# Layer 0's weighted sum by rows: which operand stays in TensorE, and the gate's second half on VectorE

## The chip, the cores and the metric

The kernel runs on one core of a Trainium2 chip. The metric is device time in microseconds (us) of one execution. A core has engines that each take their own queue of instructions in order: TensorE (PE; its weight loads are listed apart, as PEld), VectorE (DVE), ScalarE (ACT) and GpSimd (POOL). SyncE (SP) issues transfers; GpSimd can issue them too, from its own queue. TensorE writes to PSUM[...]; the other data lie in SBUF, 128 partitions wide.

## The reference

Four graph layers run on x (16 batches of 1024 nodes and 128 features) with a 0/1 adjacency matrix of 1024 by 1024 for each batch. After each, the result is added to x and normalized by rows. The change touches layer 0 alone, which for each batch computes

```
h = x @ W_w.T + W_b
e = (h @ A) @ h.T;  e = e + e.T
att = softmax(where(adj > 0, e, -9e15), axis=1) * adj
h_prime = relu(att @ h)
coeff = sigmoid([x, h_prime] @ gate_w.T + gate_b)
x = layernorm(x + coeff * x + (1 - coeff) * h_prime)
```

The gate has one number for each node: a product of 256 weights with the node's 128 features of x and its 128 features of h_prime. Layer 1 thins the adjacency row by row (the dilation, a sequential process of eight column blocks here) and runs three aggregation steps; layer 2 is an attention like layer 0 with three gates; layer 3 is two graph convolutions. A general path, taken where the inputs are not what the fast path assumes, stands behind a flag and is not run.

## The kernel before, in words

The fast path is `fast_kernel`. Layer 0 has three generators for each batch:

- `before` (L922) loads x as `xn` (eight blocks of 128 nodes, nodes on partitions) and the adjacency by rows as `an`, turns it into an fp8 copy `Y` on ScalarE, checks its symmetry on VectorE against TensorE's turned copy (L943, L944), turns x into `xT` (features on partitions), and makes `G` (for the scores), `hn` (h by rows) and `gx` (the gate's product with x, by way of `gates`, L769). Its last step stores Y from GpSimd (L965).
- `attention` (L967) goes through eight blocks `jt` of 128 neighbours: scores by `wide_matmul` (L724), mask and extreme on VectorE (L983), exp on ScalarE (L985), then `hs`, the block of h divided by the sum of exp (L989). One step later `weigh` (L970) adds the block to `acc`. Here hs is the operand that is loaded into TensorE, and em, the exp's 1024 columns, is moved through it in two halves of 512. The result is h_prime turned: features on partitions, nodes along the columns.
- `after` (L998) takes the ReLU into `hpT`, forms the gate's product with it in `gates` (four matmuls, a copy by ScalarE, two turns), the tanh that stands for the sigmoid, then xn times its factor, hpT turned back to rows by eight transposes (`turned`, L754) and times its factor, their sum, and `normed` (L787): statistics on VectorE, the power -1/2 on GpSimd (L745), scale and shift on ScalarE (L801). GpSimd then stores the result (L1019).

`in_rounds` (L815) sets the order in which the three are written: a `yield n` puts the generator's next piece n rounds later. In iteration b run `before` of batch b+1, `attention` of b and `after` of b-1 together, in about 18 rounds. The written order isn't the order on the engines: a scheduler orders each engine's instructions before the run, with the written order as priority and its own estimate of when each is ready. What is written later may therefore come earlier where its engine is free.

Buffers: three for xn, so that the load of batch b+1 takes the place of batch b-2 and must wait until that has been stored; three for an; two each for the scores' PSUM tile and for em; one for acc, which ReLU must have read before the next batch's first sum; two PSUM banks (`ps_h`) for all small products and turns. All loads of x and of the adjacency go out on SP's queue.

After layer 0 comes the dilation, in which `prepare`, `fixed_point` and `removal` alternate. Its small tiles are in the pool `dl_small`. Layer 0's last `after` runs beside its first steps, and L1188, the power -1/2 of the node degrees on GpSimd, is ready as soon as the last scores are.

Of the kernel before, what the change touches and what calls it, by code (L numbers as in the profile page):

```python
# [9 lines left out]
F32 = mybir.dt.float32  # L10
# [5 lines left out]
FP8 = mybir.dt.float8e4  # L16
# [6 lines left out]
P = 128  # L23
# [616 lines left out]
def fast_kernel(ctx: ExitStack, tc: tile.TileContext, t: dict, out: bass.AP, flag: bass.AP):  # L640
# [46 lines left out]
    def nat(ap):  # L687
        return ap.rearrange("(t p) d -> p t d", p=P)
# [39 lines left out]
    def tiles3(ap):  # L728
        return ap.rearrange("p (t d) -> p t d", d=P)
# [53 lines left out]
    def half_rows(v):  # L783

        return v[:, :, None].to_broadcast([P, 4, P])
# [124 lines left out]
    work = ending.enter_context(tc.tile_pool(name="l0_work", bufs=1, reuse_waits="tile"))  # L910
    small = ending.enter_context(tc.tile_pool(name="l0_small", bufs=2, reuse_waits="tile"))
    b0 = row_bcast(wts, t["L0_gnn_W_b"], P, "l0brow")
    gw = wts.tile([P, 2, 32], F32, name="l0gw")
    nc.vector.memset(gw, 0.0)
    with nc.allow_non_contiguous_dma(reason="a vector of 256"):
        nc.sync.dma_start(gw[:, :, 0], t["L0_gnn_gate_w"].rearrange("o (h d) -> d (o h)", d=P))
    gb = row_bcast(wts, t["L0_gnn_gate_b"], 1, "l0gb")
    gbh = wts.tile([P, 1], F32, name="l0gbh")
    nbig = wts.tile([P, 1], F32, name="l0nbig")
# [2 lines left out]
    def before(s, b):  # L922

        s.xn = work.tile([P, NT, P], F32, name="xn", bufs=3)
        nc.sync.dma_start(s.xn, nat(t["x"][b]))
        yield 1
        for it in range(NT):
            c = b * NT + it
# [22 lines left out]
            if it == (4 if b else 1):  # L951
                s.G = work.tile([P, N], F32, name="G", bufs=2)
                for p, c in products(ps_h, (M0, s.xT)):
                    nc.scalar.activation(s.G[:, c], p, AF.Identity, scale=-1.0, bias=nu)
                pz = gates(ps_h, early.tile([P, N], FP8, name="chk").bitcast(F32), (gw[:, 0, :], s.xT))
                s.gx = small.tile([P, NT], F32, name="gx")
                nc.vector.tensor_copy(s.gx.rearrange("p (q t) -> p q t", t=2), pz[:, :, :, 0])
            if it == (5 if b else 2):
# [8 lines left out]
    def attention(s, b):  # L967
        s.acc = ps_a.tile([P, N], F32, name="acc")

        def weigh(jt, hs, em):  # L970
            for h in range(H2):
                c = slice(h * 512, (h + 1) * 512)
                nc.tensor.matmul(s.acc[:, c], hs, em[:, c], start=(jt == 0), stop=(jt == NT - 1))  # L973

        for jt in range(NT):
            js = slice(jt * P, (jt + 1) * P)
            c = b * NT + jt
            mn = mx0[:, c:c + 1]
            msk = work.tile([P, N], BF16, name="msk", bufs=2)
            nc.scalar.activation(msk, Y[b][:, jt, :], AF.Identity, scale=-BIG, bias=nbig)  # L980
            e = wide_matmul(ps_w, s.G[:, js], s.xT)
            em = work.tile([P, N], F32, name="em", bufs=2)
            nc.vector.tensor_tensor_reduce(em, e, msk, 1.0, 3.0e38, op0=OP.add, op1=OP.min, accum_out=mn)  # L983
            sm = small.tile([P, 1], F32, name="sm")
            nc.scalar.activation(em, em, AF.Exp, scale=-1.0, bias=mn, accum_out=sm)  # L985
            rs = small.tile([P, 1], F32, name="rs")
            nc.vector.reciprocal(rs, sm)
            hs = small.tile([P, P], F32, name="hs")
            nc.vector.tensor_scalar(hs, s.hn[:, js], rs, None, op0=OP.mult)  # L989
            yield  # L990
            if jt:
                weigh(*late)
            late = jt, hs, em
            yield
        weigh(*late)
        yield

    def after(s, b):  # L998

        hpT = work.tile([P, N], F32, name="hpT")  # L1000
        nc.scalar.activation(hpT, s.acc, AF.Relu)
        yield 3
        pz = gates(ps_h, work.tile([P, NT, P], F32, name="r").rearrange("p t d -> p (t d)")[:, :N // 4], (gw[:, 1, :], hpT))
        co = small.tile([P, NT], F32, name="co")
        nc.vector.tensor_add(co.rearrange("p (q t) -> p q t", t=2), pz[:, :, :, 0],
                             s.gx.rearrange("p (q t) -> p q t", t=2))
        nc.scalar.activation(co, co, AF.Tanh, scale=0.5, bias=gbh)
        cx = small.tile([P, NT], F32, name="cx")
        nc.vector.tensor_scalar(cx, co, 0.5, 1.5, op0=OP.mult, op1=OP.add)
        nc.vector.tensor_scalar(co, co, -0.5, 0.5, op0=OP.mult, op1=OP.add)  # L1010
        yield 3
        r = work.tile([P, NT, P], F32, name="r")
        nc.vector.tensor_mul(s.xn, s.xn, per_row(cx))
        for p, c, k in turned(ps_h, hpT):
            nc.vector.tensor_mul(r[:, k, :], tiles3(p), half_rows(co[:, k]))
        nc.vector.tensor_add(s.xn, s.xn, r)
        yield 4
        normed(small, s.xn)
        nc.gpsimd.dma_start(nat(x1_d[b]), s.xn)  # L1019
        yield  # L1020
# [13 lines left out]

    with ExitStack() as ph:
        sb = ph.enter_context(tc.tile_pool(name="dl_sb", bufs=2, side="right", reuse_waits="tile"))
        tiny = ph.enter_context(tc.tile_pool(name="dl_small", bufs=3, side="right", reuse_waits="tile"))
        ps_b = ph.enter_context(tc.tile_pool(name="dl_pb", bufs=1, space=PSUM, side="right", reuse_waits="tile"))
        ps_d = ph.enter_context(tc.tile_pool(name="dl_pd", bufs=1, space=PSUM, side="right", reuse_waits="tile"))
        ps_s = ph.enter_context(tc.tile_pool(name="dl_ps", bufs=2, space=PSUM, side="right", reuse_waits="tile"))  # L1040
# [826 lines left out]
```

## Time and profile before

| | |
|---|---|
| median of 3 runs | 2696.75 us (2693.25 to 2697.32) |
| the profiled execution | 2694.93 us; its span 2693.2 us |
| TensorE busy, of the span | 2539.0 us (94%) |
| VectorE | 2085.4 us (77%) |
| ScalarE | 1977.5 us (73%) |
| GpSimd | 317.7 us (12%) |
| layer 0: first to last record of its sums (L973) | 27.8 to 624.3 us |
| dilation: first and last column write (L1157) | 649.8 to 1001.2 us |
| layer 1's aggregations (L1307), first to last | 1005.7 to 1562.7 us |
| layers 2 and 3 (L1679, L1619) | from 1692.8 us to the end |
| mean granted TensorE clock | 0.983 of full speed |

The profile lists instructions by source line; a line can be a helper's, so L759 is every transpose by `turned`, and the names (out<-in) tell which. A float32 matmul appears as two records. The busy time of a matmul reaches to its modelled end, which overlaps its successor; the distance from one start to the next is what it costs the queue. A note in square brackets is idle time of the engine before the instruction, with what ended it. Stages have different limits, so the share of the whole span says little of one stage.

### The profile page before, as it was taken

How to read it: one execution, taken by the hardware profiler on the slowest of the kernel's cores; microseconds unless marked ns; L12 is line 12 of the kernel's file. 1: busy time of each engine (PE TensorE's matmuls, PEld its weight loads, DVE VectorE, ACT ScalarE, POOL GpSimd, SP SyncE). 2: the span in 40 equal slices, each digit the busy share in tenths (PEclk: the TensorE clock that was granted, in tenths of full speed). 3: DMA queues.
4: the chain of work that ended last, by engine and by line, in shares of the span. 5: the costliest groups of instructions: out<-in, count | busy, mean ns of one | idle time of the engine just before them, and what ended most of it. 6: DMA issues, size and time to landing. Idle time of an engine off the chain costs nothing.

```text
span 2693.2 us, 41450 instructions
## 1 busy us (share of the span) xinstructions
PE 2539.0 (94%) x14888; PEld 1677.9 (62%) x14888; DVE 2085.4 (77%) x5590; ACT 1977.5 (73%) x3188; POOL 317.7 (12%) x287
## 2 busy tenths in 40 slices
PE   8999999997888869999999998999999999999986
PEld 4444454444666648887788885566566666666655
DVE  6887778876898877777688875678778777887885
ACT  7888889885988866666655534777777777777773
POOL 0000000003000001111122132001100100001010
PEclk9999999998999989999999998999999999999998
DMA  6555555530000052233366673102122111111100
GB/s 191 157 180 172 164 172 168 168 121 21 2 3 2 2 212 87 95 118 128 132 230 238 228 263 132 40 32 79 67 85 77 63 63 63 63 63 63 47 24 25
DMA packets 120807, 285.34 MB, mean 106 GB/s; under 512 B 12304, under 2 KB 65424, under 8 KB 113424
## 3 DMA queue, kind: packets, MB, share of 16 engines
q1 hardware_dynamic: 101280, 203.33, 23.1%
q0 software_dynamic: 19312, 79.28, 7.6%
q8 instruction: 119, 1.95, 0.3%
q14 instruction: 96, 0.79, 0.1%
HBM read 202.72 MB, written 79.82 MB: 105 GB/s over the span
## 4 chain that ended last, share of the span: by engine, by line
PE 58%; DVE 16%; issue 6%; ACT 4%; POOL 4%; DMA 2%; POOLq 0%; ACTq 0%; DVEq 0%
PE ph L1619 8%; PE acc L1679 7%; PE acc L1307 7%; PE ph L766 5%; PE acc L973 5%; PE pmm L724 5%; PE ph L759 4%; PE ph L1433 4%; PE pmm L1691 3%; PE ph L1606 2%; DVE mid L1097 2%; DVE keep L1148 2%; POOL ln_rstd L745 1%; POOL rn L745 1%; ACT q L1145 1%
## 5 line engine op out<-in xcount | busy, mean ns | idle before, releaser
L745 POOL TENSOR_TENSOR ln_rstd<-ln_rstd,mhalf 128x8 f32<-128x8 f32 (+1 forms) x68 | 108.3, 1593 | 1318.7 <-DVE ln_rstd L742 864.2
L973 PE MATMUL acc<-em,hs 128*128 128x512 f32 x512 | 259.3, 607 | 2.5 <-DVE past L1075 1.3
L724 PE MATMUL pmm<-xT,G 128*128 128x512 f32 x512 | 259.8, 604 | 0.0
L1679 PE MATMUL acc<-ex,hs 128*128 128x512 f32 x512 | 248.9, 596 | 7.5 <-DVE hs L1706 4.6
L801 ACT ACTIVATE xn<-xn,ln_nb,ln_rstd 128x128 f32<-128x128 f32 x512 | 204.6, 481 | 61.1 <-DVE ln_nb L799 61.0
L1307 PE MATMUL acc<-a,hi 128*128 128x512 f32 x768 | 232.7, 396 | 11.5 <-DVE a L1294 8.5
L1307 PE MATMUL acc<-a,lo 128*128 128x512 f32 x768 | 230.3, 394 | 5.9 <-DVE lo L1274 5.8
L985 ACT ACTIVATE em<-em,mx 128x1024 f32<-128x1024 f32 x128 | 146.3, 1143 | 54.0 <-DVE mx L983 52.7
L983 DVE CUSTOM_DVE_ANT_0 em<-pmm,msk 128x1024 f32<-128x1024 f32 x128 | 156.1, 1219 | 31.9 <-PE pmm L724 30.8
L1699 ACT ACTIVATE ex<-em,mn 128x1024 f32<-128x1024 f32 x128 | 146.9, 1148 | 44.7 <-DVE mn L1696 44.0
L1691 PE MATMUL pmm<-G,hT 128*128 128x512 f32 (+3 forms) x416 | 175.3, 523 | 0.1
L1696 DVE CUSTOM_DVE_ANT_0 em<-pmm,msk 128x1024 f32<-128x1024 f32 x128 | 155.4, 1214 | 24.4 <-PE pmm L1693 22.3
L1307 PEld LDWEIGHTS acc<-a,lo 128*128 128x128 f32 x768 | 143.1, 189 | 41.2 <-DVE lo L1274 12.0
L1307 PEld LDWEIGHTS acc<-a,hi 128*128 128x128 f32 x768 | 141.8, 189 | 42.9 <-DVE a L1294 11.0
L1157 ACT ACTIVATE carry<-pc,negone 128x1024 fp8e4<-128x1024 f32 x128 | 141.4, 1116 | 26.2 <-PE pc L1156 23.2
L931 ACT ACTIVATE carry<-an 128x1024 fp8e4<-128x1024 f32 x128 | 134.5, 1051 | 30.5 <-DMA an<-in_adj 29.7
L980 ACT ACTIVATE msk<-carry,l0nbig 128x1024 bf16<-128x1024 fp8e4 x128 | 145.4, 1136 | 0.0
L1619 PE MATMUL ph<-A,hi 128*128 128x512 f32 x512 | 143.1, 420 | 1.2 <-DVE zn L1608 0.7
L1687 ACT ACTIVATE msk<-A,nbig 128x1024 bf16<-128x1024 fp8e4 x128 | 144.2, 1137 | 0.0
L1296 ACT CAST a<-A 128x1024 fp32r<-128x1024 fp8e4 x96 | 98.4, 1048 | 54.3 <-PE acc L1307 52.7
L1679 PEld LDWEIGHTS acc<-ex,hs 128*128 128x128 f32 x512 | 88.6, 190 | 76.8 <-issue 54.6
L1296 ACT CAST a<-carry 128x1024 fp32r<-128x1024 fp8e4 x96 | 99.1, 1047 | 47.1 <-PE acc L1307 46.8
(319 smaller groups left out, 6185.2 us busy)
## 6 DMA issues: line engine op xcount, KB each, us to landing
an<-in_adj SPq DMA_DIRECT2D x128, 512.0 KB, 3.7
adj_d<-carry POOLq DMA_DIRECT2D x16, 1024.0 KB, 4.2
A<-dil_d SPq DMA_DIRECT2D x16, 1024.0 KB, 5.3
rdeg<-rdeg_d SPq DMA_DIRECT2D x32, 512.0 KB, 3.9
A<-adj_d SPq DMA_DIRECT2D x16, 1024.0 KB, 4.8
ag_d<-ag POOLq DMA_DIRECT2D x24, 512.0 KB, 5.0
ag<-ag_d SPq DMA_DIRECT2D x24, 512.0 KB, 5.3
xn<-in_x SPq DMA_DIRECT2D x16, 512.0 KB, 4.4
```

The lines of the kernel that those rows point to most:

```text
L724: nc.tensor.matmul(p[:, h * 512:(h + 1) * 512], lhsT, rhs[:, h * 512:(h + 1) * 512], start=True, stop=True)
L745: nc.gpsimd.tensor_tensor(r, r, mhalf[:, :n], op=OP.pow)
L801: nc.scalar.activation(r[:, k.start + i, :], r[:, k.start + i, :], AF.Identity, scale=rstd[:, i:i + 1], bias=nb[:, i:i + 1])
L973: nc.tensor.matmul(s.acc[:, c], hs, em[:, c], start=(jt == 0), stop=(jt == NT - 1))
L983: nc.vector.tensor_tensor_reduce(em, e, msk, 1.0, 3.0e38, op0=OP.add, op1=OP.min, accum_out=mn)
L1296: nc.scalar.copy(a, A[:, 2 * i:2 * i + 2, c])
L1307: nc.tensor.matmul(acc, part[:, jt, :], pieces[h * NT // 2 + k][:, jt - 2 * k, :], start=(part is parts[0] and jt == 0), stop=(part is par ...
L1619: nc.tensor.matmul(p, part[:, jt, :], A[jt][:, c], start=(jt == 0 and i == 0), stop=(jt == NT - 1 and i == 1))
L1679: nc.tensor.matmul(s.acc[:, c], hs, ex[:, c], start=(jt == 0), stop=(jt == NT - 1))
L1691: nc.tensor.matmul(e[:, c], s.hT[:, js], s.G[:, c], start=True, stop=True)
L1696: nc.vector.tensor_tensor_reduce(row, e, msk, 1.0, 0.0, op0=OP.add, op1=OP.min, accum_out=mn)
L1699: nc.scalar.activation(ex, row, AF.Exp, scale=-1.0, bias=mn, accum_out=sm)
```

## The change

- `weigh` swaps the operands: each of the eight 128-column blocks of em is loaded into TensorE and hs (128 columns) is moved through it. The sum comes out by rows: nodes on partitions, eight blocks of 128 features. The first of each four blocks in a PSUM bank carries the start flag of the bank.
- `after` takes the ReLU by rows into `hp`. The gate's half is a product with `ghrow` (the 128 weights, repeated on all partitions) and a sum along the features, on VectorE. Gate matmuls, copy and turns for h_prime are gone. hp is multiplied by its factor in SBUF, at full width.
- The pieces of `after` stand at rounds 0, 6, 9 and 17 in place of 0, 3, 6 and 10.
- From batch 3 on, x is loaded from GpSimd's queue.
- The gate's columns in `gw` are only x's; `ghrow` is one more load. Pool `dl_small` has two buffers of each tile in place of three.

```diff
-    gw = wts.tile([P, 2, 32], F32, name="l0gw")
+    gw = wts.tile([P, 32], F32, name="l0gw")
     nc.vector.memset(gw, 0.0)
-    with nc.allow_non_contiguous_dma(reason="a vector of 256"):
-        nc.sync.dma_start(gw[:, :, 0], t["L0_gnn_gate_w"].rearrange("o (h d) -> d (o h)", d=P))
+    nc.sync.dma_start(gw[:, 0:1], t["L0_gnn_gate_w"][:, :P].rearrange("o d -> d o"))
+    ghrow = row_bcast(wts, t["L0_gnn_gate_w"][:, P:], P, "l0gh")
...
-        nc.sync.dma_start(s.xn, nat(t["x"][b]))
+        (nc.gpsimd if b > 2 else nc.sync).dma_start(s.xn, nat(t["x"][b]))
...
-                pz = gates(ps_h, early.tile([P, N], FP8, name="chk").bitcast(F32), (gw[:, 0, :], s.xT))
+                pz = gates(ps_h, early.tile([P, N], FP8, name="chk").bitcast(F32), (gw, s.xT))
...
         def weigh(jt, hs, em):
-            for h in range(H2):
-                c = slice(h * 512, (h + 1) * 512)
-                nc.tensor.matmul(s.acc[:, c], hs, em[:, c], start=(jt == 0), stop=(jt == NT - 1))
+            for k in range(NT):
+                c = slice(k * P, (k + 1) * P)
+                nc.tensor.matmul(s.acc[:, c], em[:, c], hs, start=(jt == 0 and k % 4 == 0), stop=(jt == NT - 1 and k % 4 == 3))
...
     def after(s, b):

-        hpT = work.tile([P, N], F32, name="hpT")
-        nc.scalar.activation(hpT, s.acc, AF.Relu)
-        yield 3
-        pz = gates(ps_h, work.tile([P, NT, P], F32, name="r").rearrange("p t d -> p (t d)")[:, :N // 4], (gw[:, 1, :], hpT))
+        hp = work.tile([P, NT, P], F32, name="hp")
+        nc.scalar.activation(hp, tiles3(s.acc), AF.Relu)
+        yield 6
+        r = work.tile([P, NT, P], F32, name="r")
+        nc.vector.tensor_tensor(r, hp, per_col(ghrow), op=OP.mult)
         co = small.tile([P, NT], F32, name="co")
-        nc.vector.tensor_add(co.rearrange("p (q t) -> p q t", t=2), pz[:, :, :, 0],
-                             s.gx.rearrange("p (q t) -> p q t", t=2))
+        nc.vector.tensor_reduce(co, r, AX.X, OP.add)
+        nc.vector.tensor_add(co, co, s.gx)
         nc.scalar.activation(co, co, AF.Tanh, scale=0.5, bias=gbh)
         cx = small.tile([P, NT], F32, name="cx")
         nc.vector.tensor_scalar(cx, co, 0.5, 1.5, op0=OP.mult, op1=OP.add)
         nc.vector.tensor_scalar(co, co, -0.5, 0.5, op0=OP.mult, op1=OP.add)
         yield 3
-        r = work.tile([P, NT, P], F32, name="r")
         nc.vector.tensor_mul(s.xn, s.xn, per_row(cx))
-        for p, c, k in turned(ps_h, hpT):
-            nc.vector.tensor_mul(r[:, k, :], tiles3(p), half_rows(co[:, k]))
-        nc.vector.tensor_add(s.xn, s.xn, r)
-        yield 4
+        nc.vector.tensor_mul(hp, hp, per_row(co))
+        nc.vector.tensor_add(s.xn, s.xn, hp)
+        yield 8
         normed(small, s.xn)
         nc.gpsimd.dma_start(nat(x1_d[b]), s.xn)
...
-        tiny = ph.enter_context(tc.tile_pool(name="dl_small", bufs=3, side="right", reuse_waits="tile"))
+        tiny = ph.enter_context(tc.tile_pool(name="dl_small", bufs=2, side="right", reuse_waits="tile"))
```

## The prediction

> **What bounds the kernel now.** I read the page first: span 2693.2 us, TensorE busy 94% of it. Only layer 0 is edited, so I cut its steady part into windows of one batch (columns: window, length, then busy us and instruction count of PE, weight loads, DVE, ACT, POOL, then clock, DMA share, GB/s):
>
> ```profile
> 287.55:325.10 37.55, 37.55 (x158) 18.54 (x157) 30.20 (x100) 33.23 (x56) 3.16 (x3) 1.00 0.54 168
> 325.10:362.65 37.55, 37.55 (x158) 18.45 (x157) 30.23 (x99) 33.42 (x56) 3.17 (x3) 1.00 0.51 168
> ```
>
> TensorE has no idle time at full clock; ScalarE is at 89%, VectorE at 80%, DMA at half. From about 62 to 610 us the kernel goes at TensorE's pace, 37.55 us a batch. As matmul ends are modelled, I price by starts, from TensorE's timeline of one batch (start, busy, line, group, count):
>
> ```profile
> 318.46 1.08 PE L973 MATMUL acc<-em,hs 128*128 128x512 f32 x2
> 319.37 1.95 PE L962 MATMUL ph<-l0WT,xT 128*128 128x128 f32 x16
> 321.16 1.02 PE L973 MATMUL acc<-em,hs 128*128 128x512 f32 x2
> 322.02 1.88 PE L724 MATMUL pmm<-xT,G 128*128 128x512 f32 x4
> 323.73 1.88 PE L973 MATMUL acc<-em,hs 128*128 128x512 f32 x4
> 325.45 1.88 PE L724 MATMUL pmm<-xT,G 128*128 128x512 f32 x4
> ...
> 335.70 0.64 PE L775 MATMUL pq<-hpT,l0gw 128*32 128x256 f32 x8
> 336.26 1.12 PE L724 MATMUL pmm<-xT,G 128*128 128x512 f32 x2
> 337.23 0.38 PE L780 MATMUL pg<-identf,r 128*128 128x128 f32 x2
> 337.45 0.28 PE L943 MATMUL pt<-identb,carry 128*128 128x128 bf16 x2
> ...
> 341.13 0.60 PE L759 MATMUL ph<-identf,hpT 128*128 128x128 f32 x4
> 341.57 1.02 PE L724 MATMUL pmm<-xT,G 128*128 128x512 f32 x2
> 342.43 0.60 PE L759 MATMUL ph<-identf,hpT 128*128 128x128 f32 x4
> 342.87 1.02 PE L973 MATMUL acc<-em,hs 128*128 128x512 f32 x2
> ```
>
> No row carries an idle note: each starts when the one before lets it. One float32 matmul is two records. Third, the POOL timeline, for what the later normalization and x's queue touch:
>
> ```profile
> 351.37 1.66 POOL L745 TENSOR_TENSOR ln_rstd<-ln_rstd,mhalf 128x8 f32<-128x8 f32 x1 [30.03 <-DVE ln_rstd L742]
> 353.59 0.60 POOL L965 DMA_DIRECT2D adj_d<-carry  x1 [0.56 <-ACT chk L777]
> 358.08 0.91 POOL L1019 DMA_DIRECT2D x_d<-xn  x1 [3.88 <-ACT xn L801]
> ...
> 624.10 20.74 POOL L1188 TENSOR_TENSOR deg<-deg,mhalf 128x128 f32<-128x128 f32 x1 [5.87 <-DVE deg L1187]
> 644.82 1.63 POOL L745 TENSOR_TENSOR ln_rstd<-ln_rstd,mhalf 128x8 f32<-128x8 f32 x1
> ```
>
> POOL is nearly idle in the steady part. At the layer's end the power of the degrees holds it for 20.7 us, and the last normalization waits behind.
>
> **What the Trainium skill says.** "TensorE: Matmul & The Clock Gate", section LDWEIGHTS: a load costs by its columns, about 107 ns for 128. One 128-column float32 pass starts every 1.79/16 = 112 ns in L962, with a load for each pass: the trace agrees that the load hides behind the pass, just. "VectorE: DVE Perf Modes", the perf-mode tier table: float32 tensor_tensor and tensor_reduce run at 1x; the trace agrees, 1.22 us for the 1024-wide products. "DMA: Bandwidth & Descriptors", latency table: a DMA issued from GpSimd has its first byte at about 1 us instead of 0.6; here POOL's 512 KB stores land 4.2 us after issue and SP's 512 KB x loads 4.4, so a load by POOL should take about as long, plus 0.9 us of issue against 0.38.
>
> **The change part by part, per batch.**
>
> Weighted sum by rows. Before, each of 8 blocks has 2 matmuls of 512 columns: 4 records in 325.45 - 323.73 = 1.72 us. After, 8 matmuls of 128 columns with a new weight block each: 16 records in exactly L962's shape, 321.16 - 319.37 = 1.79 us. Added: 8 x 0.07 = 0.56 us. Bounds: 0 if loads hide wholly; if they didn't hide, 16 x 8 x 0.107 = 13.7 us, which L962 excludes. The start flag on every fourth block costs nothing.
>
> Removed from TensorE, from the same timeline: the gate products of hpT, 336.26 - 335.70 = 0.56; the two turns of their output, 337.45 - 337.23 = 0.22; the eight turns of hpT, 2 x 0.44 = 0.88; and the slower matmul after the gate (337.23 - 336.26 = 0.97 against 0.86) 0.11. Sum 1.77 us. Net -1.21 us, so 36.34 us.
>
> Fifteen batches (0 to 14) do this inside the saturated stretch: 15 x 1.21 = 18.2 us.
>
> VectorE: two products from PSUM go (2 x 0.683). In come a product (as L1013, 1.218), a sum over 1024 (not shown; the 512-wide one at L1444 is 0.679, so at most 1.36), the product by co (1.22) and an 8-wide add in the old one's place: about +2.4 us, to 32.6 of 36.3, 90%. ScalarE loses the 0.356 us copy: 33.0, 91%. Neither overtakes TensorE, which covers both; were VectorE the bound, the 2.4 us would be a loss.
>
> Later normalization (rounds 10 to 17 of about 18) and x by POOL. The store follows the normalization, and the x load three batches on waits for that store. Now the store issues at 358.08, the load on SP at 362.33, it lands at 366.7, and the transposes of that xn begin one period after 338.47, at 376.0: 9.3 us of slack. Seven rounds of 37.55/18 are 14.6 us, so in the worst case x lands 5.3 us late, plus 0.5 for the issue. But rounds are priorities, not times: L1188, written after two removal steps, runs at 624 before any. Idle VectorE slots will take the small normalization earlier. And TensorE has scores, sums and adjacency turns that need no xn; G is wanted only in the next batch. I take 0. On SP the wait would hold up adjacency loads; on POOL only the next store of Y and power queue behind, some 25 us later, so the move costs SP and ScalarE nothing. For batches 0 to 2 nothing waits for a buffer.
>
> Start: ghrow is one more DMA on SP before x and the adjacency, +0.43 us; the gate's column load has half the elements. I count +0.4. The dl_small pool at 2 buffers: every tile is last read by VectorE, TensorE or ScalarE before its second successor, so 0; bounds 0 and +1.
>
> Layer's end: VectorE stands idle 5.8 us at L799 until POOL gives the last ln_rstd, which is fixed by L1188. The extra 2.4 us of VectorE work there falls into that wait: 0, between -5.8 (planner separates them) and +2.4.
>
> I allow 0.2 us a batch, 3 us in all, of new stalls on TensorE, since VectorE's queue is fuller between scores and exp. This is a choice; bounds 0 and 0.8 a batch.
>
> Sum against the profiled execution: 2694.93 - 18.2 + 0.4 + 3.0 = 2680.1. The median of the runs lies 1.8 us above that execution: 2682.
>
> **Rivals.**
> *VectorE and ScalarE take the pace.* At 90% each, with waits for DMA on ScalarE besides (29.7 us in the waits on an), order may cost 0.8 us a batch: gain 15 x 0.4 = 6, 2691. For: both fuller. Against: scores have two PSUM buffers, and each block has 4.5 us.
> *x comes late (the slower side).* TensorE takes its queue in order; if xn's transposes sit where the plan expected x and the chip delivers later, it stands before the transposes of xn in the 13 batches (3 to 15) that load by POOL. It decides at 18.2/13 = 1.4 us of lateness each; at 3 us, 2694.9 - 18.2 + 39 = 2716, or 2718 by the median. For: the slack of 9.3 us is smaller than the shift of 14.6. Against: no wait of TensorE on a load in layer 0 now.
> *The power of the degrees traps batch 14's normalization.* If its ln_rstd falls behind L1188, VectorE stands from about 628 instead of 640.7, 13 us: 2695. Against: VectorE has gaps from 611 to 622 for it.
> *No effect:* if records hid a non-TensorE pace, 2697; the gapless starts speak against.
>
> **How the numbers follow.** Main case 0.60, its own range 2676 to 2689. Shared pace 0.12, x late 0.20, trapped normalization 0.04, no effect 0.04. The measurement can tell about 0.2%, 5.4 us. Faster: main, half of shared pace (0.06), a fifth of x late (0.04): 0.70. Slower: the rest of x late: 0.16. Same: half of shared pace, the trap, no effect: 0.14. The range begins at 2672 (no new stalls, the 5.8 us wait gone) and reaches to 2701 (x late by about 1.7 us in each of the 13 batches, 22 us).
>
> **What would show it.** Right: windows of 36.2 to 36.6 us a batch in layer 0, TensorE still gapless, sixteen acc records in about 1.79 us, no L775 on hpT. Wrong: idle notes on TensorE before xn's transposes or before the sums (from VectorE's hs); sixteen records well above 1.8 us; layers after 650 us changing length by more than 2 us; POOL holding the x load far into the batch.

## The result, and the profile after

| | before | after |
|---|---|---|
| median of the runs | 2696.61 us (2689.99 to 2702.22) | 2701.24 us (2694.53 to 2706.40) |
| span of the profiled execution | 2693.2 us | 2695.8 us |
| one batch, mean of eight in layer 0 | 37.55 us | 37.96 us |
| TensorE's work in it, idle time taken off | 37.54 us | 36.90 us |
| the same with every record at its usual distance (estimate, below) | 37.50 us | 36.41 us |
| start of the power of the degrees | 624.10 us | 628.05 us |
| from there to the end | 2069.1 us | 2067.8 us |

The ratio is 1.0017, 95% interval 1.0008 to 1.0025: the change made the kernel slower, by less than the 0.2% named in the prediction as the limit of what counts. 2682 us was forecast.

TensorE's work did fall, but a batch did not get shorter. Here are stretches of the kernel after (columns as in the prediction), two batches from the middle and a late one:

```profile
328.90:366.80 37.90, 36.87 (x234) 25.63 (x232) 31.89 (x100) 32.88 (x55) 4.08 (x4) 1.00 0.49 163
366.80:404.70 37.90, 36.83 (x232) 25.74 (x232) 31.94 (x98) 32.48 (x56) 4.06 (x4) 1.00 0.50 167
...
558.80:600.07 41.27, 38.53 (x238) 27.50 (x236) 32.35 (x100) 32.08 (x54) 4.07 (x4) 0.96 0.47 151
```

TensorE is busy 36.9 of 37.9 us: it has idle time now. VectorE went from 30.2 to 31.9 us. The batch at 558.8 takes 41.3 us, with a clock of 0.96. TensorE's timeline of one batch:

```profile
331.73 1.94 PE L724 MATMUL pmm<-xT,G 128*128 128x512 f32 x4
333.99 0.23 PE L943 MATMUL pt<-identb,carry 128*128 128x128 bf16 x1 [0.33 <-ACT carry L931]
334.06 2.00 PE L973 MATMUL acc<-hs,em 128*128 128x128 f32 x16
...
340.41 0.60 PE L759 MATMUL ph<-identf,xn 128*128 128x128 f32 x4
341.21 0.38 PE L943 MATMUL pt<-identb,carry 128*128 128x128 bf16 x4 [0.21 <-ACT xT L950]
341.44 1.94 PE L724 MATMUL pmm<-xT,G 128*128 128x512 f32 x4
343.21 1.95 PE L973 MATMUL acc<-hs,em 128*128 128x128 f32 x16
344.99 0.44 PE L943 MATMUL pt<-identb,carry 128*128 128x128 bf16 x5
...
362.84 1.02 PE L724 MATMUL pmm<-xT,G 128*128 128x512 f32 x2
364.25 0.91 PE L973 MATMUL acc<-hs,em 128*128 128x128 f32 x6 [0.39 <-DVE hs L989]
364.99 0.39 PE L943 MATMUL pt<-identb,carry 128*128 128x128 bf16 x4
365.21 0.44 PE L973 MATMUL acc<-hs,em 128*128 128x128 f32 x2
365.49 0.33 PE L943 MATMUL pt<-identb,carry 128*128 128x128 bf16 x3
365.66 0.89 PE L973 MATMUL acc<-hs,em 128*128 128x128 f32 x6
```

An unbroken block of sixteen sum records costs 344.99 - 343.21 = 1.78 us, as forecast. But two things are new. Blocks are broken in other ways: from 364.25 on, one stands as six, two, six and two records between transposes of the adjacency. And there are idle notes, with different releasers: ScalarE's copy of an adjacency block, its copy of xT, VectorE's hs.

How far did the work fall? By idle notes alone, 0.64 us a batch. But an idle note starts at the modelled end of the matmul before it, and elsewhere that end overlaps the successor. Four score records take 323.73 - 322.02 = 1.71 us in the kernel before; from 331.73 on they take 333.99 - 331.73 - 0.33 = 1.93 us with the note taken off. So an idle note leaves some 0.2 us in "work" in which TensorE stood. With the usual distance put in for every record before idle time (an estimate from the trace), the work is 36.41 us, 1.09 less than before, and TensorE stands for 1.55 us a batch in place of the 1.06 of the notes.

The waits of ScalarE between 170 and 520 us (us in total, times, longest) say what is late; first before, then after:

```profile
ACT em L985 <- DVE mx L983: 32.1, 35, 2.0
ACT carry L931 <- DMA an<-in_adj: 8.1, 18, 0.6
```

```profile
ACT carry L931 <- DMA an<-in_adj: 41.7, 27, 2.7
ACT hp L1001 <- PE acc L973: 2.7, 10, 0.3
ACT em L985 <- DVE mx L983: 1.8, 9, 0.2
```

ScalarE, which before waited for VectorE's scores, now waits for adjacency loads. Last, the POOL timeline:

```profile
356.41 1.66 POOL L745 TENSOR_TENSOR ln_rstd<-ln_rstd,mhalf 128x8 f32<-128x8 f32 x1 [0.27 <-DVE ln_rstd L742]
365.54 0.96 POOL L1018 DMA_DIRECT2D x_d<-xn  x1 [7.46 <-ACT xn L801]
370.94 0.89 POOL L925 DMA_DIRECT2D xn<-in_x  x1 [4.45 <-DMA x_d<-xn]
...
628.05 20.74 POOL L1187 TENSOR_TENSOR deg<-deg,mhalf 128x128 f32<-128x128 f32 x1 [1.62 <-DVE deg L1186]
```

The store of x comes at 365.5, 37 us after the ReLU of its batch (328.9), where it came 27 us after it. The load of x then starts 2 to 4 us after the next ReLU, 367.1, where it started 5 to 6 us before, and falls into the batch's run of adjacency loads. Between 170 and 520 us it lands after 5.8 us (median), before after 4.3.

### The profile page after: what moved, and what is told of

Read it like the earlier page. It is cut to its first block, busy times and chain, and to the rows that moved or that the text cites. A ratio compares the mean times of both kernels' runs of the same rounds, so it can differ in the third digit from the quotient of the medians.

```text
span 2695.8 us, 43880 instructions
## 1 busy us (share of the span) xinstructions
PE 2527.4 (94%) x16136; PEld 1800.6 (67%) x16136; DVE 2115.9 (78%) x5606; ACT 1970.0 (73%) x3172; POOL 330.3 (12%) x300
## 4 chain that ended last, share of the span: by engine, by line
PE 51%; DVE 17%; ACT 11%; DMA 8%; issue 7%; POOL 4%; SPq 0%; POOLq 0%; ACTq 0%; DVEq 0%
PE ph L1618 8%; PE acc L1678 7%; PE acc L1306 7%; PE ph L766 5%; DMA an<-in_adj 5%; PE ph L1432 4%; PE ph L759 4%; PE acc L973 3%; PE pmm L1690 3%; ACT em L985 3%; PE ph L1605 2%; PE pmm L724 2%; DVE mid L1096 2%; ACT msk L980 2%; DVE keep L1147 2%
## 5 line engine op out<-in xcount | busy, mean ns | idle before, releaser
L973 PEld LDWEIGHTS acc<-hs,em 128*128 128x128 f32 x2048 | 251.4, 194 | 42.3 <-issue 24.3
L973 PE MATMUL acc<-hs,em 128*128 128x128 f32 x2048 | 274.5, 282 | 1.9 <-DVE hs L989 1.5
L724 PE MATMUL pmm<-xT,G 128*128 128x512 f32 x512 | 250.3, 603 | 0.3 <-DVE mx L983 0.3
```

The costliest lines, as they stand in the source:

```text
L724: nc.tensor.matmul(p[:, h * 512:(h + 1) * 512], lhsT, rhs[:, h * 512:(h + 1) * 512], start=True, stop=True)
L973: nc.tensor.matmul(s.acc[:, c], em[:, c], hs, start=(jt == 0 and k % 4 == 0), stop=(jt == NT - 1 and k % 4 == 3))
```

## The experiments

"Period" is the mean time between ReLUs over eight batches, "work" is TensorE's in it: distances from start to start without idle time. It is too high by what stands before idle notes, as above: with usual distances it is 37.90 us in e13, 36.41 in e3 and e6, 36.30 in e16 and e18. In e4, e14 and e15 it includes stretches at half clock. Each ratio is to runs of the kernel before that were taken beside that run.

| kernel | median, us | ratio to before | period | work |
|---|---|---|---|---|
| old rounds (e1) | 2714.56 | 1.0079 [1.0062, 1.0096] | 39.10 | 37.63 |
| old rounds, x on SP (e2) | 2714.61 | 1.0071 [1.0054, 1.0087] | 39.17 | 37.67 |
| no product (e3) | 2691.81 | 0.9986 [0.9977, 0.9995] | 37.53 | 36.69 |
| before with late rounds (e4) | 2787.32 | 1.0340 [1.0323, 1.0358] | 45.25 | 39.97 |
| swap alone (e5) | 2724.81 | 1.0106 [1.0090, 1.0123] | 39.81 | 38.96 |
| old rounds, no product (e6) | 2695.95 | 0.9996 [0.9988, 1.0005] | 37.29 | 36.67 |
| after, x on SP (e7) | 2702.89 | 1.0023 [1.0014, 1.0033] | 38.34 | 36.56 |
| product on GpSimd (e8) | 2716.02 | 1.0073 [1.0056, 1.0090] | 38.06 | 36.79 |
| old sum, rest changed (e9) | 2705.09 | 1.0038 [1.0025, 1.0050] | 38.61 | 36.45 |
| old operands, eight pieces (e10) | 2726.81 | 1.0114 [1.0097, 1.0131] | 39.82 | 38.95 |
| swap alone, unsplit (e11) | 3114.06 | 1.1550 [1.1531, 1.1570] | | |
| after, unsplit (e12) | 3101.92 | 1.1510 [1.1491, 1.1530] | | |
| swap, order of before (e13) | 2703.85 | 1.0026 [1.0017, 1.0036] | 38.37 | 38.05 |
| after, order of before (e14) | 2732.16 | 1.0125 [1.0108, 1.0142] | 40.15 | 37.60 |
| old sum, order of before (e15) | 2726.52 | 1.0111 [1.0093, 1.0128] | 39.58 | 36.94 |
| e14 without product (e16) | 2692.33 | 0.9987 [0.9978, 0.9996] | 37.30 | 36.73 |
| gate work moved (e17) | 2706.10 | 1.0039 [1.0025, 1.0054] | 38.05 | 36.98 |
| e16, fourth buffer (e18) | 2686.15 | 0.9959 [0.9945, 0.9972] | 37.01 | 36.79 |

What a run isolates depends on the scheduler (called the planner below), which orders every kernel anew. In the traces, up to 580 us, TensorE, VectorE and ScalarE have the same order in e1 and e2, in e5 and e10, in the changed kernel and e7 (but for five places near the start), and, as to the work they share, in the runs held to the order of the kernel before (e13 to e16, e18). The orders of e3, e6, e8 and e9 differ from those of the kernels that they were made from, so each of them shows its edit and a new order together.

### Rounds, queue and product

The first four runs: the old places of `after`'s pieces (e1), also x on SP (e2), the changed kernel without VectorE's gate work (e3), and the kernel before with the late places and x on GpSimd (e4).

```diff
 e1   -        yield 6        +        yield 3
      -        yield 8        +        yield 4
 e3   -        nc.vector.tensor_tensor(r, hp, per_col(ghrow), op=OP.mult)
      -        nc.vector.tensor_reduce(co, r, AX.X, OP.add)
      -        nc.vector.tensor_add(co, co, s.gx)
      +        nc.vector.tensor_scalar(co, s.gx, 1.0, None, op0=OP.mult)
 e4   (before) -        yield 3        +        yield 6
      (before) -        yield 4        +        yield 8
```

> The changed kernel with the pieces of after back at rounds 0, 3, 6 and 10 (x stays on GpSimd's queue). Theory A (collision: the later normalization puts x's store and load into the burst of adjacency loads, these land late, ScalarE waits for them in order, TensorE starves): x leaves before the burst again, adjacency loads land in about 3.6 us, ScalarE's waits on an fall from 61 to some 20 us, the period from 37.9 to 36.5-36.9 us; 2680 to 2688. Theory B (VectorE's extra 2.4 us a batch delay the checks and the sums): no gain, 2695 to 2703.

> The changed kernel with the old rounds and x on SP's queue for all batches: only the sums by rows, the gate on VectorE and the small pool are left of the change. Theory A: the best of the row forms, 2678 to 2688, period 36.4 to 36.8. Theory B: as the changed kernel or worse, 2695 to 2705. If it is like e1, the queue itself does not matter.

> The changed kernel without the product and the sum on VectorE (leaves out h_prime's half of the gate, so the gate sees x alone). 2.4 us a batch less on VectorE, everything else in place. Theory A: little change, 2694 to 2702, adjacency loads still land in 4.4 us and more while x is on its way. Theory B: the gain comes back, 2678 to 2686.

> The kernel before, with the pieces of after at rounds 0, 6, 9 and 17 and x on GpSimd's queue from batch 3 on: the moved part alone, no rows. Theory A: slower than before by 5 to 20 us (2702 to 2717), idle notes on TensorE, adjacency loads late. Theory B: no difference, 2694 to 2700, since VectorE has no more to do.

All four runs lie outside both theories' ranges. The old rounds made the changed kernel 13 us slower (e1); so its late rounds, with the order that came of them, were worth 13 us. e1 and e2 agree, so the queue of x makes no difference there. e3 is 9.4 us faster than the changed kernel, but in a new order, so how much of that is VectorE's gate work isn't shown; leaving it out does not bring 2680. e4 shows the danger of a late x at its full size, far beyond Theory A: TensorE waits 36.5 us for x between 170 and 520 us, up to 6.7 us at a time.

### The swap alone, the queue again, GpSimd

e5 is the kernel before with only `weigh` changed; e6 is e2 without product and sum; e7 the changed kernel with x on SP; e8 has the product on GpSimd.

```diff
 e5   (before) weigh as in the change, nothing else
 e8   -        nc.vector.tensor_tensor(r, hp, per_col(ghrow), op=OP.mult)
      +        nc.gpsimd.tensor_tensor(r, hp, per_col(ghrow), op=OP.mult)
```

> Edit: the kernel before with the operand swap in weigh alone; the sum by rows is then taken as if it were turned, so h_prime is wrong, but every later instruction has the shape and place it had. Theory A (TensorE sets the pace of the kernel before, so its added time is paid in full): the sums went from 14.29 to 14.98 us a batch in the traces, +0.69 us, times 15 = +10 us over before: 2703 to 2709, period 38.1 to 38.4, TensorE still without idle time. Rival B (the pace of before is already shared with VectorE and ScalarE, so 0.7 us of TensorE hides): within 3 us of before, period below 37.8. Rival C (VectorE's hs, a small tile needed by the moving side late, brings new stalls): more than 15 us slower, with idle notes before the sums.

> Edit: the changed kernel with the pieces of after at their old rounds, x on SP, and without the gate's product and sum on VectorE (the gate takes x's half alone). Theory A (at the old rounds it is the amount of VectorE work in the middle of the batch that starves TensorE): 2.44 us of VectorE less, so the period falls from 39.1 to 37.4 or below, 2680 to 2692. Rival B (what costs is that the full-width product, sum and normalization stand so early, whatever the gate costs): within 8 us of the 2714.6 of the run with the product.

> Edit: the changed kernel, with x loaded from SP's queue again; the late rounds stay. Theory A (the late rounds make x's load wait for a late store, and only GpSimd's queue keeps that wait from the adjacency loads): SP stands for the store and the adjacency loads behind it go out late: 2710 to 2730. Rival B (the queue makes no difference here either, as at the old rounds; the load comes late in both, and the loss lies in the load's time, not in its queue): within 4 us of the changed kernel's 2701.

> Edit: the changed kernel with the gate's product (128x1024) on GpSimd in place of VectorE; the sum stays on VectorE. Theory A (VectorE's load is what costs, half of what leaving out product and sum gave): 2692 to 2698, VectorE 1.2 us a batch less. Rival B (latency counts: GpSimd takes longer than VectorE's 1.22 us, so tanh, the normalization, the store and the load of x all come later): 2701 or more, with longer waits of TensorE for xn.

e5 is the surprise: an edit priced at 0.6 to 0.7 us a batch costs 28.5 us, 2.3 us a batch in its trace. That is Rival C's size, not its sign: from 170 to 520 us TensorE waits 0.2 us for hs and 5.9 us, before turns of the adjacency, for VectorE's copy of gx. e6 is 18.7 us faster than e2, a fall of Theory A's kind though the time stays 4 us above its range, and in a new order; it ends where the kernel before ends, though TensorE has 1.1 us a batch less to do. e7 ties with the changed kernel (Rival B): the queue of x cost nothing and won nothing.

e8 is slower, as Rival B said, but not for its reason. Its batches take 38.06 us, 0.1 more than the changed kernel's, its last ReLU comes 1.1 us later, and TensorE has no wait for xn between 170 and 520 us. The loss lies at the layer's end: the last batch's product stands in GpSimd's queue behind the power of the degrees, and VectorE stands for it.

```profile
629.81 20.75 POOL L1187 TENSOR_TENSOR deg<-deg,mhalf 128x128 f32<-128x128 f32 x1 [4.61 <-DVE deg L1186]
650.53 2.33 POOL L1004 TENSOR_TENSOR r<-hp,l0gh 128x1024 f32<-128x1024 f32 x1
```

```profile
652.90 1.22 DVE L1006 TENSOR_REDUCE co<-r 128x8 f32<-128x1024 f32 x1 [19.95 <-POOL r L1004]
```

The dilation's first column write comes at 672.7 us, in the changed kernel at 653.7. So e8 decides nothing about the batches.

### Is it the operands, or the order?

e9 is the changed kernel with the old sum. e10 keeps the old operands and cuts the moving side into eight pieces of 128. e11 and e12 make the eight matmuls one unit for the planner.

```diff
 e9   weigh as before, the rest as in the change
 e10  (before) -            for h in range(H2):
      (before) -                c = slice(h * 512, (h + 1) * 512)
      (before) +            for h in range(NT):
      (before) +                c = slice(h * P, (h + 1) * P)
      ...                        # start and stop flags once for each four pieces
 e11, e12      +            with tc.tile_critical():   # around weigh's loop
```

> Edit: the changed kernel with the old sum (hs loaded, em moving in two halves of 512); everything else as changed. The sum then comes out turned and is taken as rows, so h_prime is wrong; the work after it has its shapes and places. Theory A (the operand swap is what eats the gain: alone it cost 28.5 us; without it the 1.66 us of TensorE a batch are won): period 36.0 to 36.4, 2668 to 2682. Rival B (VectorE's fuller queue and the late x bound the changed kernel whatever the sum costs): period 37.5 or more, 2693 to 2703.

> Edit: the kernel before, hs still loaded and em still moving, but in eight pieces of 128 columns in place of two of 512; the result is the same. Theory A (what costs in the swap is the count of short instructions, which the planner spreads in small runs among other work): most of the swap's loss, 2712 to 2728, the sums at 15 us a batch or more. Rival B (what costs is that em, not hs, is loaded for each pass): within 4 us of before, the sums at about 14.4.

> Edit: the operand swap alone as in the earlier run of it, but the eight matmuls of a block are one unit for the planner, so that nothing comes between them. h_prime is wrong as there. Theory A (the splitting of a block's sums between transposes and other small work is what raises 16 records from 1.79 to 1.95 us and brings the idle time): sums 14.3 to 14.6 us a batch, period 37.7 to 38.2, 2699 to 2708. Rival B (the loss comes with the swap itself, wherever the matmuls stand): 2718 or more.

> Edit: the changed kernel with the eight matmuls of a block as one unit for the planner. Theory A (splitting): sums from 14.98 to 14.3-14.6 us a batch and less idle time, 2688 to 2696. Rival B (the pace lies with VectorE, ScalarE and the loads, and TensorE's saved time turns into idle time): 2699 to 2705. Rival C (a unit must wait for all its inputs and holds small work up behind it): above 2706.

e10 decides. hs stays loaded as before, and the loss is the same as with em loaded. The planner put the instructions of e5 and e10 in the same order on every engine, one for one, and the profiles can hardly be told apart. One batch of each, e5 and then e10:

```profile
301.69:341.45 39.76, 38.94 (x253) 27.48 (x252) 30.16 (x99) 33.26 (x56) 3.16 (x3) 1.00 0.47 159
```

```profile
301.69:341.45 39.76, 38.91 (x253) 27.42 (x252) 30.14 (x99) 33.24 (x56) 3.17 (x3) 1.00 0.50 160
```

So which operand is loaded doesn't matter. What both share, against the kernel before, is short matmuls and the order that came of them: the sums stand in 20 runs a batch in place of 13 (in the changed kernel in 14).

e11 and e12 don't tell splitting from swap. The unit brings waits of its own, as this line of e12's waits of TensorE shows: sums stand for adjacency loads that they don't read.

```profile
PE acc L974 <- DMA an<-in_adj: 38.4, 12, 5.6
```

e9 lies 2 us above Rival B's range and far from Theory A's. Without the swap the rest of the change loses 8 us too, and the changed kernel, which adds the swap, is 4 us faster than that. The parts don't add up, as they would if each had a price; e9 has an order of its own.

### The same work in the order of the kernel before

For these runs each engine's and queue's instructions of layer 0 are tied to one another in a given order, without waits. ORDER is a packed text with the names of the instructions, queue by queue, in the order of the kernel before; new instructions stand where those stood whose place they take.

```diff
+    def in_order(text):
...
+        by = {i.name: i for i in nc.cur_bb.bb.instructions}
+        info = mybir.DependencyInfo(mybir.DependencyClass.NoSync, mybir.DependencyReason.DATA)
+        for queue in zlib.decompress(base64.b64decode(text)).decode().split(";"):
+            names = [f"I-{n}" for n in queue.split() if f"I-{n}" in by]
+            for a, b in zip(names, names[1:]):
+                tc.add_manual_dep(by[b], a, info, reason="order")
+
+    in_order(ORDER)
     scores.close()
```

> Edit: the operand swap alone (h_prime wrong, as in the earlier run of it), with the instructions of layer 0 held, on every engine and queue, in the order of the kernel before; the eight short matmuls of a block stand where its two long ones stood, four for each. Theory A (the swap's 28.5 us came from the order that the planner makes out of short matmuls): only the short matmuls' own 0.56 to 0.69 us a batch are left, period 38.1 to 38.3, 2703 to 2709. Rival B (short matmuls cost that much wherever they stand): 2718 or more.

> Edit: the changed kernel with x on SP, layer 0's instructions held in the order of the kernel before on every engine and queue: the gate's product, sum and addition stand where the addition of the gate's halves stood, the product by the factor where the first of the two old ones stood, what is gone is left out. Theory A (the order is what ate the gain): TensorE's work of 36.3 to 36.9 us a batch sets the period again, 2678 to 2690. Rival B (VectorE's 2.4 us more in the middle of the batch delay scores and checks in this order too): TensorE waits for VectorE, 2697 or more.

> Edit: as the run before this one, but with the old sum (hs loaded, two halves of 512; h_prime wrong). Theory A (order): period 35.8 to 36.3, 2668 to 2679. Rival B (VectorE's load): TensorE has still less work and waits all the more; within 5 us of the run with the sum by rows.

e13 confirms Theory A: in the order of the kernel before, the swap costs 7.8 us by the medians, 0.52 us a batch over fifteen batches. Its trace is of one of its longer executions (span 2708.9 us): 38.37 us a batch, just above Theory A's range and 0.8 more than before, 0.3 of it idle time. The other 21 us of e5 were the order. One batch of e13 with no idle time on TensorE, 0.34 us longer than before:

```profile
336.87:374.76 37.89, 37.89 (x254) 27.22 (x254) 30.20 (x98) 33.26 (x58) 3.17 (x3) 1.00 0.51 167
```

e14 falls to Rival B: the whole change in that order is 28 us slower than the swap. Its waits of TensorE, then of ScalarE, from 170 to 520 us:

```profile
PE ph L759 <- DVE chk L944: 15.5, 8, 2.2
PE pt L943 <- ACT carry L931: 3.8, 9, 1.3
```

```profile
ACT em L985 <- DVE mx L983: 34.2, 33, 2.0
ACT co L1008 <- DVE co L1007: 18.3, 9, 2.2
```

ScalarE stands 2 us in each batch for the gate's sum, at its tanh; TensorE stands 2 us before xn's transposes, for a bank of `ps_h` that VectorE's check must free. e15 comes close to Rival B, which said within 5 us: with the old sum TensorE's work is 0.7 us a batch less (0.4 of it because the clock was at half speed for less time), and the run is only 5.6 us faster. VectorE in the kernel before shows why these 2.4 us find no room. Two stretches of one batch (the third of the engines' columns is VectorE), and some lines of its timeline:

```profile
328.30:351.10 22.80, 22.80 (x98) 11.18 (x96) 22.18 (x75) 20.38 (x33) 0.00 (x0) 1.00 0.48 158
351.10:365.80 14.70, 14.70 (x61) 7.22 (x60) 8.00 (x25) 13.03 (x24) 3.17 (x3) 1.00 0.54 184
```

```profile
339.51 1.22 DVE L1013 TENSOR_TENSOR xn<-xn,cx 128x1024 f32<-128x1024 f32 x1
340.64 0.15 DVE L987 RECIPROCAL rs<-sm 128x1 f32<-128x1 f32 x1
340.71 0.67 DVE L936 SCALAR_TENSOR_TENSOR chk<-an 128x512 fp8e4<-128x512 f32 x1
...
354.73 0.17 DVE L987 RECIPROCAL rs<-sm 128x1 f32<-128x1 f32 x1 [1.50 <-ACT em L985]
...
359.98 0.16 DVE L987 RECIPROCAL rs<-sm 128x1 f32<-128x1 f32 x1 [1.92 <-ACT em L985]
```

From 328.3 to 351.1 us VectorE is busy for 22.2 of 22.8 us: scores, both checks of the adjacency, the mixing of x and h_prime and the statistics stand nearly end to start. Its idle time lies between 351 and 366. "80% busy" was full for some 60% of a batch and about half empty for the rest, and in e14 the gate's product and sum were put into the full part. In the changed kernel's own order they stand there too, and the full part, which ended 20 us after the ReLU (330.7), lasts until 27 us after it (328.9):

```profile
333.65 1.22 DVE L1004 TENSOR_TENSOR r<-hp,l0gh 128x1024 f32<-128x1024 f32 x1
338.98 1.22 DVE L1006 TENSOR_REDUCE co<-r 128x8 f32<-128x1024 f32 x1
...
356.80 1.22 DVE L983 CUSTOM_DVE_ANT_0 em<-pmm,msk 128x1024 f32<-128x1024 f32 x1 [0.54 <-PE pmm L724]
```

### How far would better places bring it?

e16 is e14 without product and sum. In e17 VectorE's gate and mixing work stands in the stretch that was idle, and the normalization works one batch later. e18 is e16 with one more adjacency buffer.

```diff
 e17  -        s.xn = work.tile([P, NT, P], F32, name="xn", bufs=3)
      +        s.xn = work.tile([P, NT, P], F32, name="xn", bufs=4)
      ...                # product and sum:
      +        for k in range(NT):
      +            nc.vector.scalar_tensor_tensor(r, hp[:, k, :], 1.0, ghrow, op0=OP.mult, op1=OP.mult, accum_out=co[:, k:k + 1], saturate=False)
      ...
                         # product by co, and sum with xn:
      +        for k in range(NT):
      +            nc.vector.scalar_tensor_tensor(s.xn[:, k, :], hp[:, k, :], co[:, k:k + 1], s.xn[:, k, :], op0=OP.mult, op1=OP.add)
 e18  -            an = early.tile([P, N], F32, name="an", bufs=3)
      +            an = early.tile([P, N], F32, name="an", bufs=4)
```

> Edit: the changed kernel in the order of the kernel before, with the gate's product and sum on VectorE left out (the gate takes x's half alone, so the output is a little off). Theory A (in this order it is the 2.44 us of product and sum, put into the stretch where VectorE has no idle time, that costs 28 us against the swap alone): VectorE has what it had before, TensorE 1.2 us less: period 36.4 to 37.0, 2676 to 2690. Rival B (it is the three full-width operations on x and hp, or h_prime's path without TensorE, that hold VectorE up): period 38.5 or more, above 2708.

> Edit: the changed kernel in the order of the kernel before, but VectorE's gate and mixing work stands in the last third of the batch, where VectorE was idle for 6.9 us in the kernel before: product with sum as eight 128-column operations, the product of x, and factor times hp plus x as eight 128-column operations; the normalization keeps its place and works on the batch before. x has four buffers, the gate's x half three. Theory A (place and order decide, not the amount: VectorE's full stretch is shorter than before by about 4 us, the rest fits the idle one): TensorE sets the pace at 36.3 to 37.0 us a batch, 2674 to 2690, faster than both kernels. Rival B (the last third has no room either: exp and scores wait there on VectorE one after the other): period 37.5 or more, 2697 or more.

> Edit: the run without the gate's product and sum in the order of the kernel before, with four buffers for the adjacency's rows in place of three (room comes from the product's tile, which is not needed there). Without the fourth buffer TensorE had 36.73 us of work in 37.30 us a batch, 0.5 us of idle time, most of it before transposes that wait for ScalarE's copy of a row block that was loaded late. Theory A (the ring of three buffers is the limit next to TensorE: a load goes out when VectorE has checked the block three before): idle time below 0.2 us, period 36.7 to 37.0, 2682 to 2689. Rival B (VectorE's stretch without idle time is the limit itself, with the loads early or late): period 37.2 or more, 2690 to 2696.

e16 lies between its theories, 2 us above Theory A's range: without product and sum e14's 40.15 us a batch become 37.30, and 2732 us become 2692, with the rest of the order the same. So 2.44 us of work in VectorE's full stretch cost 2.85 us a batch. About 0.85 us of that is TensorE's clock (an estimate: half of 4 x 3.4 us over eight batches): in e14's eight batches it was at half speed for four stretches of 3.4 us, at waits of some 2 us, in e16's never. e17: the gate work is all there, and moved it costs 26 us less than in e14. So the place decides more than the amount, but the result is Rival B's range: 10 us slower than the kernel before. In its trace some 5 us of the loss come after the last batch: the power of the degrees starts 4.2 us after the last ReLU, in the kernel before 0.8 us ahead of it. Two batches of e17:

```profile
297.70:335.42 37.72, 36.96 (x236) 25.98 (x236) 32.25 (x119) 33.00 (x57) 3.16 (x3) 1.00 0.49 168
335.42:374.34 38.92, 36.95 (x236) 25.98 (x236) 32.23 (x119) 32.88 (x57) 3.16 (x3) 1.00 0.49 163
```

The second has an idle note of 1.34 us before a transpose, for ScalarE's copy of an adjacency block. e16 has such notes too, 3.9 us over nine batches, and its ScalarE waits for loads:

```profile
ACT em L985 <- DVE mx L983: 32.0, 29, 2.0
ACT carry L931 <- DMA an<-in_adj: 8.4, 13, 1.6
```

With a fourth buffer (e18) ScalarE's waits for loads are gone, and TensorE has no wait left that the profile lists:

```profile
ACT em L985 <- DVE mx L983: 37.3, 38, 2.0
ACT co L1005 <- DVE co L1004: 3.1, 10, 0.3
```

```profile
288.31:325.32 37.01, 36.78 (x236) 25.97 (x236) 29.96 (x97) 32.81 (x57) 3.16 (x3) 1.00 0.51 171
```

In this order the ring of three adjacency buffers was the limit next to TensorE's, at 37.3 us a batch, only 0.25 us below the 37.55 of the kernel before (Theory A; the period is 0.01 us above its range, since 0.2 us of idle time stay). In three orders without h_prime's product and sum on VectorE (e3, e6, e16) the period stood between 37.29 and 37.53, with 36.67 to 36.73 us of work. An estimate from these: with three buffers even a gate that cost VectorE nothing would hardly have won more than 15 x 0.26 = 4 us; a better order isn't ruled out.

No run that does the whole computation beat the kernel before. e3, e6, e16 and e18 leave out h_prime's half of the gate; e5, e9, e11, e13 and e15 take the sum in the wrong layout.

## Why the prediction was wrong, point by point

**The sum by rows, 0.56 us a batch.** The price of the instructions was about right: 0.52 us by e13's median, 0.34 in its batch without idle time, and the same whichever operand is loaded (e10). The loads hide behind the passes as said, though a load record of 128 float32 columns lasts 190 ns in the trace before, not the 107 that the prediction took for its upper bound. What failed was the silent part of the step, that sixteen short records stand where four long ones stood. The scheduler makes its order anew from the instructions that it gets; alone, the swap cost 2.3 us a batch.

**What TensorE loses, 1.77 us.** The three removed groups measured 1.66 us a batch in the trace before (0.57, 0.22, 0.87), and they are gone. The sums took 0.67 us more in the changed kernel. With usual distances before idle notes the work fell by 1.09 us, where 1.21 were forecast, to 36.41 us for 36.34; that it came so close is partly luck, since the turns of the adjacency took 0.17 us less. So TensorE's side of the sum held.

**"Neither overtakes TensorE, which covers both."** This step failed. It compared busy times over a batch (VectorE 90%, ScalarE 91%), but cover has to hold in each stretch. VectorE was full from 328 to 351 us, and the added work went there, in e14 and in the changed kernel. In the order of the kernel before it cost 2.85 us a batch there (e14 against e16), through scores and checks, PSUM banks and the gate's tanh; and without it the ring of three adjacency buffers left TensorE 0.25 us of room a batch, not the 1.21 that the forecast wanted. The 0.2 us allowed for new stalls measured 1.06 by idle notes and some 1.5 with what stands before them.

**Later normalization and x on GpSimd, 0.** Not nothing: with the old rounds the changed kernel was 13 us slower (e1). But the slack of 9.3 us was nearly used up: x was loaded some 8.6 us later in the batch, amid the adjacency loads. In most batches TensorE hardly waited for it, but the last two periods of the stretch took 39.9 and 41.3 us, 5.4 us together over the usual 37.9. In the second TensorE stands for x (1.71 us), in the first for an adjacency block (1.97 us), and after both its clock is at half speed for 3.4 us. The rival "x comes late" was right in kind and small in size; e4 shows the size it can have. The move to GpSimd's queue was worth nothing either way (e1 and e2, e7).

**Start and end of the layer.** The first ReLU came 0.36 us later, 0.4 was forecast. The power of the degrees did not trap batch 14's normalization, which stood at 617 us, and from the power's start to the end of the kernel the profile after is 1.3 us shorter, within the bounds of -5.8 to +2.4. `dl_small` shows no cost there.

**The rivals.** "VectorE and ScalarE take the pace" is the one that held, with the loads behind them. It was given 0.8 us a batch and a chance of 0.12. The period shows 37.96 us, 36.41 of work and 1.55 of standing, where 36.34 and 0.2 were forecast. The power of the degrees did trap work in one run, e8's last product.

What stays open: how much of the changed kernel's own loss lies in its order and how much in VectorE's load. The runs show each alone to be large (21 us in e5 against e13; 28 us in e14 against e13), and that they don't add. No run holds the changed kernel's own order and takes VectorE's work out of it: e3 leaves out product and sum and is 9.4 us faster, but in another order. A fourth adjacency buffer together with the whole change wasn't tried; e18 took its room from the product's tile, and e17 gave that room to a fourth buffer of x.

## What to carry to other kernels

Where a scheduler orders the instructions, an edit that changes their number or length buys a new order, and that order can cost more than the edit; hold the old order to see what the work itself costs. Before calling work "hidden", find the stretch of the batch where it will stand, and see in the timeline of its engine whether there is idle time there. A gapless engine is a limit, not the only one: ask how far behind the second limit is, here a ring of three buffers 0.25 us back, before counting on more than that. And before explaining a run by its batches, see where in its trace the time was lost (e8).

## What the runs showed of the hardware

A wait of TensorE of under 2 us could cost more than its length. The kernel after, TensorE's timeline, and the stretch behind the wait (the clock is the third number from the end):

```profile
569.81 0.63 PE L759 MATMUL ph<-identf,xn 128*128 128x128 f32 x4 [1.71 <-DMA xn<-in_x]
570.27 3.15 PE L973 MATMUL acc<-hs,em 128*128 128x128 f32 x14
573.21 1.29 PE L724 MATMUL pmm<-xT,G 128*128 128x512 f32 x2
574.34 0.60 PE L759 MATMUL ph<-identf,xn 128*128 128x128 f32 x4
```

```profile
570.28:573.69 3.41, 3.41 (x17) 3.27 (x16) 0.69 (x3) 3.41 (x6) 0.00 (x0) 0.51 0.48 169
```

After 1.71 us of idle time fourteen records take 573.21 - 570.27 = 2.94 us, where 1.56 are usual, and the next two 1.13 where 0.86 are: some 1.65 us lost on top. The Trainium skill, "TensorE: Matmul & The Clock Gate", section "Why this matters for your kernels", says that a gap over about 3 us returns the clock to half. Here the clock fell after 1.7 and 2.0 us, each time for 3.4 us; the measurement decides for this case. It didn't fall with every such gap: between 100 and 600 us, with eight of e14's eleven gaps of 1.8 to 2.2 us and two of e15's thirteen of 1.5 to 2.2, not with 1.7 us in e7, nor with 2.6 us in e3. Gaps of 0.2 to 0.4 us show no such thing.

GpSimd took 2.68 us for a product of 128x1024 float32, VectorE 1.22. Eight VectorE operations of 128 columns with a sum each started every 0.33 us, 2.7 us in all, no less than the full-width product and sum together (2.44).
